# Where layer 1 of the first image stands in the order of emission: alone after layer 0, or in the second stream beside layer 0 of the next image

## The chip, the cores and the metric

The kernel runs on one core of one Trainium2 chip. A core has five engines with a queue of instructions each: TensorE (PE: matmuls, with weight loads as PEld), VectorE (DVE), ScalarE (ACT), GpSimd (POOL) and SyncE (SP), which here only starts transfers. The metric is the device time of one execution in microseconds (us); less is better. The time of a kernel is the median over its runs.

## The reference, cut to what matters

Four images of 48 channels and 256 x 256 pixels, all in float32, go through four layers. Each layer normalises its input over groups of three channels of the whole image (`_gn`), computes a branch and adds it to its input:

```python
x = x + _L0_conv_ref(_gn(x), ...)   # 1x1 and 3x3 conv to 288 channels, products of 8x8 spectra, layer norm, gate, 1x1 conv
x = x + _L1_conv_ref(_gn(x), ...)   # 1x1 conv to 288, mask on 8x8 spectra, 3x3 depthwise conv, gelu gate, 1x1 conv
x = x + _L2_conv_ref(_gn(x), ...)   # cumulative sums over the image, read at four corners of a box per pixel (gather)
x = x + _L3_conv_ref(_gn(x), ...)   # 1x1 and 3x3 conv to 192, gelu gate, 1x1 conv, mask on 8x8 spectra
```

The statistics of `_gn` cover a whole image, so a layer of one image can start only when the layer before of the same image has ended. Images do not depend on each other.

## The kernel before

**Two streams.** The work is a set of Python generators, one for each layer of each image (`layer0` to `layer3`), which emit instructions and `yield` a cost in planned units after each piece. `Net.run` holds two lists, `todo["a"]` and `todo["b"]`, and two planned clocks, `at["a"]` and `at["b"]`. It always advances the stream whose clock is behind and adds the yielded cost. So the emission is a zip of the two streams by planned cost. Stream a has the first statistics of image 0, then layers 0 and 1 of images 0, 1, 2, 3, then layer 3 of the four images. Stream b has the preparation of weights (`patch_weights`, `taps`), the first statistics of images 1 to 3, then layer 2 of the four images. A generator starts when its predecessors on the same image are done.

By the yields, layer 0 costs 1806 units (128 pieces, called units of layer 0 below, of two times 7), layer 1 costs 1429, layer 2 costs 3220, of which 316 are the sums and the first two pieces and the rest 33 pieces of four steps of 22 units, layer 3 costs 1080. Layer 2 of image 0 needs layer 1 of image 0, so stream b stands still while stream a emits layer 1 of image 0: that layer has the chip to itself. From then on layer 2 of image i lies beside layers 0 and 1 of image i+1, 3220 units against 3235, and layer 2 of image 3 beside layer 3 of images 0 to 2; layer 3 of image 3 (`layer3_pairs`) follows alone.

**What sets the order on an engine.** The emitted instructions go through a scheduler, which may move them within an engine by their priorities and its own estimate of times; an instruction passed to `self.pinned` (`keep_in_program_order`) keeps its place in the order of emission. After that each engine takes its instructions in order, and waits on semaphores for operands and for free buffers.

**Buffers.** Matmul results go to banks of PSUM. Stream a rotates through five banks of the pool `psa`, stream b through two of `psb`; one more bank (tag `w4`) holds the weights of the four corners in layer 2. Stream b allocates its SBUF tiles from the other side than stream a.

**Queues of transfers.** `self.dma` (line 238) starts the transfers of stream a on SP and those of stream b on POOL, where the gathers of layer 2 (line 1126, 16 a step) stand too. Layer 1 also starts many of its own on SP directly, pinned.

**Layer 0** makes, for each unit, 12 matmuls of 128 x 128 by 288 columns (line 399) and 4 of the rest of the rows (line 407) into four banks, copies them to `qkv` on ACT (line 483, four copies a unit), multiplies by the Fourier matrices (lines 491, 506), scales (lines 511 to 538), turns (line 544) and projects (line 556).

**Layer 1** has three passes. The first makes, for each of 16 strips, 32 matmuls of 49 rows by 288 columns (line 713), and copies each to the tile `hs` of which one strip (4608 KB) is stored to DRAM (`hD`). The copy is on DVE for every fourth result and on ACT for the others:

```python
if h and b % 2:
    nc.vector.tensor_copy(hs[:, :, h, b], ps[:, :288])
else:
    nc.scalar.copy(hs[:, :, h, b], ps[:, :288])
```

The second pass has 36 groups of eight channels: it loads a group (`hg`), makes the rims (line 771), sends them to neighbours by transfers (`yh<-yb`), and convolves and gates (lines 788, 794, 799, 800). The third turns back (line 865) and projects (line 877).

**Layer 2** makes the cumulative sums (lines 947, 968) and then 128 steps, each with half a piece of a 3 x 3 convolution (lines 1020, 1029), a projection (line 1045), 16 gathers (line 1126) into one of three tiles `V`, and their weighing and folding on DVE (lines 1138, 1146, 1148).

Of the kernel before, what the change touches and what calls it, by code (L numbers as in the profile page):

```python
# [192 lines left out]
class Net:  # L193
    def __init__(self, ctx, tc, a, out):
        self.tc, self.nc, self.a, self.out = tc, tc.nc, a, out
        self.nimage = a["x"].shape[0] // C

        self.banks = {
            f: ctx.enter_context(tc.tile_pool(name="ps" + f, bufs=n, space=PSUM)) for f, n in (("a", 5), ("b", 2))
        }  # L200
        self.stream, self.alone, self.turns = "a", False, 0
# [25 lines left out]

    def bank(self):
        if self.alone:
            self.turns += 1  # L230
# [160 lines left out]
    def convolve2(self, AB, W, n, j, to):  # L391
# [5 lines left out]
        def full(q, b):  # L397
            for g in range(3):
                nc.tensor.matmul(  # L399
                    to(q, b), A[:, j + half * q, 128 * b + g : 128 * b + g + 128], W[:, g, :],  # L400
                    start=b == 0 and g == 0, stop=b == 1 and g == 2,
                )

        def tails(b):
            for q in range(2):
                p = slice(64 * q, 64 * q + 58)
                nc.tensor.matmul(  # L407
                    to(q, b), B[p, j, 128 * b : 128 * b + 128], W[p, 3, :], start=b == 1, stop=b == 0
                )

# [31 lines left out]
    def layer0(self, x, mr, y, xb):  # L442
        nc, a = self.nc, self.a
        st = self.stat.tile([112, 129, 6], F32, name=self.nm("st"), tag="st" + self.stream, bufs=1)
        with ExitStack() as ctx:
# [39 lines left out]
            def spectra(t):  # L485
                t.t = []
                for f, c in ((self.fq, 0), (self.fk, 96)):
                    banks = [self.bank() for _ in range(2)]
                    for h in range(2):
                        p = slice(64 * h, 64 * h + 64)  # L490
                        nc.tensor.matmul(v3(banks[h]), f[p], t.qkv[p, :, c : c + 96], start=True, stop=True)  # L491
                    for h in range(2):
# [6 lines left out]
            def inverse(t):  # L499
# [5 lines left out]
                for h in range(2):  # L505
                    nc.tensor.matmul(po[64 * h : 64 * h + 64, 0:384], self.back[:, 0:64], t.t[h][:], start=True, stop=True)  # L506
                nc.scalar.copy(  # L507
# [33 lines left out]
            def turn(t):  # L541
                pt = self.bank()
                for b in range(4):
                    nc.tensor.transpose(pt[:96, 128 * b : 128 * b + 128], t.un[:, b, :], self.ident[:])
                t.u = sb.tile([96, 512], F32, name="u", tag=f"u{t.i}{t.j}", bufs=1)
                nc.scalar.copy(t.u[:], pt[:96, :])

            def project(t, other):
# [5 lines left out]
                for i, of in ((0, other), (1, t)):  # L554
                    n = 48 if i else 64
                    nc.tensor.matmul(pp[64 * i : 64 * i + n, :], pr[:, 0:n], of.u[:], start=True, stop=True)
                for q in range(2):
# [118 lines left out]
    def layer1(self, x, mr, y):  # L676
# [4 lines left out]
        with ExitStack() as ctx:  # L681
# [25 lines left out]
            for s in range(NS):  # L707
                xt = xts[s % 3]
                hs = sb.tile([128, 8 * NG, 2, 16], F32, name="hs", tag="hs")
                for b in range(16):  # L710
                    for h in range(2):
                        ps = self.bank()
                        nc.tensor.matmul(  # L713
                            ps[:, :288], xt[64 * h : 64 * h + 49, 128 * b : 128 * b + 128],
                            win[64 * h : 64 * h + 49], start=True, stop=True,
                        )
                        if h and b % 2:
                            nc.vector.tensor_copy(hs[:, :, h, b], ps[:, :288])
# [10 lines left out]
        with ExitStack() as ctx:  # L729
# [35 lines left out]
            def around(t):  # L765

                for e in range(4):
                    ps = self.bank()
                    for i in range(2):
                        c = 4 * i + e  # L770
                        nc.tensor.matmul(  # L771
                            ps[64 * i : 64 * i + 64, :].rearrange("p (s n) -> p s n", n=32),
                            t.wr[:, 64 * c : 64 * c + 64], t.hg[:, :, c, :], start=True, stop=True,
                        )
                    if e % 2:
# [8 lines left out]
            def gated(t, e):  # L784
                both = [self.bank() for _ in range(2)]
                for i in range(2):
                    c = 4 * i + e
                    nc.tensor.matmul(  # L788
                        both[i][:].rearrange("p (s n) -> p s n", n=32), t.wd[:, 128 * c : 128 * c + 128],
                        t.hg[:, :, c, :], start=True, stop=False,  # L790
                    )
                for i in range(2):
                    p = slice(64 * i, 64 * i + 64)
                    nc.tensor.matmul(  # L794
                        order(both[i][:]), t.wd[p, 1024 + 128 * e : 1152 + 128 * e], pick(t.yh, e)[p],
                        start=False, stop=True,
                    )
                gl = sb.tile([128, 512], F32, name="gl", tag="gl")
# [31 lines left out]
        with ExitStack() as ctx:  # L830
# [25 lines left out]
            def turn(s, j):  # L856
                gs, got = strips[s], []
                for q in range(3):
                    pt = self.bank()
                    for b in range(4):  # L860
                        if q < 2:
                            of = gs[:, 0:96, q, 4 * j + b]
                        else:
                            of = gs[:, 96:144, :, 4 * j + b].rearrange("p c h -> p (c h)")
                        nc.tensor.transpose(pt[:96, 128 * b : 128 * b + 128], of, self.ident[:])
                    gc = sb.tile([96, 512], F32, name="gc", tag=f"gc{q}")
# [4 lines left out]
            def project(s, j, got):  # L871
                xt, yt = buffers[s % 2]
                pp = self.bank()
                for last in range(2):
                    for h in range(2):
                        n = 48 if h else 64
                        nc.tensor.matmul(
                            pp[64 * h : 64 * h + n, :], pr[:, h if last else 2, 0:n], got[2 if last else h][:],
                            start=not last, stop=bool(last),
                        )  # L880
                whole = lambda t: t.rearrange("p (b r c) -> p b r c", b=4, r=8)
# [728 lines left out]
    def run(self, layers=(0, 1, 2, 3)):  # L1610
# [103 lines left out]
```

## Time and profile before

| what | value |
|---|---|
| median of 9 runs | 22758.85 us (22730.58 to 22847.83) |
| the profiled execution | 22663.54 us, span 22660.3 us |
| busy share PE, PEld, DVE, ACT, POOL | 81%, 48%, 47%, 27%, 37% |
| mean granted clock of TensorE | 0.851 |
| transfers | 3459.36 MB, mean 153 GB/s |
| layer 0 of image 0 | about 197 to 1849 us of the span |
| layer 1 of image 0, alone | about 1887 to 3056 us |
| layer 2 of image 0, first matmul of its sums to last gather | 3071 to 7549 us |
| layer 2 of image 3, last gather | 21693 us |

The profile is of one execution. A fp32 matmul of the program appears as two records on PE, so the counts of PE rows are twice those of the program. "Busy" is the time in which an engine had an instruction in work. The granted clock is the share of TensorE's full clock that the throttle granted. The chain of waits follows back from the last instruction what released what.

### The profile page before, as it was taken

What the parts mean: (1) busy time and instruction counts of PE and PEld (TensorE: products, weight loads), DVE (VectorE), ACT (ScalarE), POOL (GpSimd) and SP (SyncE); (2) the same over time, 40 slices, a digit from 0 to 9 for tenths busy, and PEclk for the clock granted to TensorE, in tenths of its full rate; (3) what the DMA queues carried; (4) which work ended last, traced back from release to release, by engine and by line L of the source; (5) the groups of instructions that cost most, each with busy time, mean ns of one, the idle gap of its engine ahead of it and who ended that gap; (6) DMA issues with size and microseconds to landing.
All of it is one profiled execution on the core that took longest, in us unless ns stands there. A gap on an engine that the chain in (4) does not pass through costs nothing.

```text
span 22660.3 us, 226381 instructions
## 1 busy us (share of the span) xinstructions
PE 18381.4 (81%) x78682; PEld 10914.8 (48%) x78682; DVE 10597.9 (47%) x23080; ACT 6045.2 (27%) x12781; POOL 8482.4 (37%) x8933
## 2 busy tenths in 40 slices
PE   8998898778777887787778877777878878877889
PEld 4564254444422544444224444442256656666678
DVE  4643244555444545554445455544443343343455
ACT  3445133333411333234113332331121111111122
POOL 1100004555444235455452354544522444444410
PEclk9998998888688988886889888868888888888889
DMA  6726863333777634336776433367864444444456
GB/s 173 165 60 226 274 200 98 100 98 96 222 249 239 187 98 103 97 97 205 247 250 191 107 101 95 97 195 245 250 204 118 106 104 108 105 106 106 105 130 150
DMA packets 1734597, 3459.36 MB, mean 153 GB/s; under 512 B 499598, under 2 KB 1273451, under 8 KB 1608600
## 3 DMA queue, kind: packets, MB, share of 16 engines
q1 hardware_dynamic: 1200800, 2149.26, 32.1%
q0 software_dynamic: 448688, 1098.99, 18.7%
q10 hardware_dynamic: 83968, 196.64, 3.4%
q8 instruction: 626, 10.26, 0.2%
q14 instruction: 515, 4.22, 0.1%
HBM read 2409.35 MB, written 832.39 MB: 143 GB/s over the span
## 4 chain that ended last, share of the span: by engine, by line
PE 61%; issue 10%; another core or an unknown queue 9%; DMA 9%; DVE 6%; ACT 2%; POOL 1%; SPq 1%; ACTq 0%; DVEq 0%; POOLq 0%
PE ps L399 19%; PE ps L1020 5%; PE ps L407 4%; PE ps L713 4%; PE ps L491 3%; PE ps L788 2%; PE ps L1045 2%; PE ps L1289 2%; DMA yh<-yb 2%; PE ps L771 2%; PE ps L794 2%; PE ps L506 2%; DVE V L1146 1%; POOL V L1126 1%
## 5 line engine op out<-in xcount | busy, mean ns | idle before, releaser
L1126 POOL DMA_INDIRECT V<-t,idx x8192 | 8049.0, 983 | 8221.5 <-DVE res L1148 4255.4
L399 PE MATMUL ps<-W,A 128*128 128x288 f32 (+1 forms) x21504 | 5464.5, 403 | 688.1 <-issue 471.7
L399 PEld LDWEIGHTS ps<-W,A 128*128 128x128 f32 x21504 | 4066.9, 205 | 2013.2 <-issue 1067.0
L1146 DVE TENSOR_TENSOR V<-V 128x1536 f32<-128x1536 f32 (+3 forms) x2048 | 1818.4, 888 | 9.2
L1138 DVE TENSOR_TENSOR V<-V,w 128x1536 f32<-128x1536 f32 x1024 | 1764.9, 1746 | 69.5 <-DMA V<-t,idx 38.0
L483 ACT COPY qkv<-ps 128x288 f32<-128x288 f32 x2048 | 759.0, 401 | 3468.1 <-PE ps L407 1085.9
L1020 PE MATMUL ps<-A,W 128*96 128x512 f32 x3072 | 1607.1, 661 | 61.3 <-issue 60.7
L511 DVE BATCH_NORM_STATS2 bs<-o 128x6 f32<-128x96 f32 x2048 | 381.7, 247 | 2443.4 <-ACT o L507 2001.1
L713 PE MATMUL ps<-win,xt 49*128 49x288 f32 x4096 | 1139.3, 610 | 405.4 <-ACT hs L720 217.6
L491 PE MATMUL ps<-qkv,c_dft_sb 64*128 64x384 f32 x4096 | 1061.4, 554 | 461.8 <-ACT qkv L483 240.1
L788 PE MATMUL ps<-hg,wd 128*128 128x512 f32 x2304 | 1217.5, 649 | 245.6 <-issue 73.2
L407 PE MATMUL ps<-W,B 58*128 58x288 f32 (+1 forms) x7168 | 1139.8, 413 | 241.0 <-issue 149.9
L1269 DVE TENSOR_TENSOR gp<-gl,ps 128x192 f32<-128x192 f32 x768 | 261.0, 351 | 2067.2 <-ACT gl L1268 1558.0
L238 POOL DMA_DIRECT2D X<-x x96 | 73.2, 763 | 2952.9 <-DMA x<-yt 2021.8
L800 DVE TENSOR_TENSOR hg<-gl,ps 128x512 f32<-128x512 f32 x576 | 394.4, 686 | 1542.6 <-ACT gl L799 815.9
L713 PEld LDWEIGHTS ps<-win,xt 49*128 49x128 f32 x4096 | 696.0, 269 | 824.1 <-ACT hs L720 406.0
L720 ACT COPY hs<-ps 128x288 f32<-128x288 f32 x1536 | 855.2, 676 | 845.4 <-PE ps L713 552.2
L1268 ACT ACTIVATE gl<-ps 128x192 f32<-128x192 f32 x768 | 246.1, 330 | 3060.0 <-PE ps L399 1318.4
L1020 PEld LDWEIGHTS ps<-A,W 128*96 128x96 f32 x3072 | 518.5, 181 | 1044.0 <-issue 1033.7
L407 PEld LDWEIGHTS ps<-W,B 58*128 58x128 f32 x7168 | 663.2, 195 | 644.9 <-issue 489.4
L794 PE MATMUL ps<-yh,wd 64*128 64x512 f32 x2304 | 741.0, 718 | 270.2 <-DMA yh<-yb 116.3
L799 ACT ACTIVATE gl<-ps 128x512 f32<-128x512 f32 x576 | 341.5, 597 | 2181.2 <-PE ps L794 1292.8
(226 smaller groups left out, 23254.0 us busy)
## 6 DMA issues: line engine op xcount, KB each, us to landing
hg<-hD SPq DMA_DIRECT2D x144, 2048.0 KB
hD<-hs SPq DMA_DIRECT2D x60, 4608.0 KB
gD<-hg SPq DMA_DIRECT2D x144, 1024.0 KB
gs<-gD SPq DMA_DIRECT2D x64, 2304.0 KB
V<-t,idx POOLq DMA_INDIRECT x8192
xt<-b SPq DMA_DIRECT2D x128, 896.0 KB
wd<-wD SPq DMA_DIRECT2D x144, 768.0 KB
A<-x SPq DMA_DIRECT2D x256, 387.0 KB
```

The source lines that it names most:

```text
L399: nc.tensor.matmul(to(q, b), A[:, j + half * q, 128 * b + g : 128 * b + g + 128], W[:, g, :], start=b == 0 and g == 0, stop=b == 1 and g == 2,
L407: nc.tensor.matmul(to(q, b), B[p, j, 128 * b : 128 * b + 128], W[p, 3, :], start=b == 1, stop=b == 0)
L483: nc.scalar.copy(t.qkv[:, 2 * q + b, :], banks[2 * b + q][:, 0:288])
L491: nc.tensor.matmul(v3(banks[h]), f[p], t.qkv[p, :, c : c + 96], start=True, stop=True)
L713: nc.tensor.matmul(ps[:, :288], xt[64 * h : 64 * h + 49, 128 * b : 128 * b + 128], win[64 * h : 64 * h + 49], start=True, stop=True,)
L720: nc.scalar.copy(hs[:, :, h, b], ps[:, :288])
L788: nc.tensor.matmul(both[i][:].rearrange("p (s n) -> p s n", n=32), t.wd[:, 128 * c : 128 * c + 128], t.hg[:, :, c, :], start=True, stop=False,
L794: nc.tensor.matmul(order(both[i][:]), t.wd[p, 1024 + 128 * e : 1152 + 128 * e], pick(t.yh, e)[p], start=False, stop=True,)
L1020: m = nc.tensor.matmul(to[q], W[:, g, :], A[:, 2 * q : 2 * q + 2, g : g + 256], start=q == 0 and g == 0, stop=q == 1 and g == 2,)
L1126: nc.gpsimd.indirect_dma_start(out=V[:, k, 4 * cr : 4 * cr + 4, :].rearrange("p e c -> p (e c)"), out_offset=None, in_=table, in_offset=ba ...
L1138: self.pinned(nc.vector.tensor_mul(Vm, Vm, wm.unsqueeze(2).to_broadcast([128, 32, 48])))
L1146: self.pinned(nc.vector.tensor_add(V[:, :, 0:n, :], V[:, :, 0:n, :], V[:, :, n : 2 * n, :]))
```

## The change

Layer 1 of image 0 moves from stream a to stream b, ahead of layer 2. Its planned cost is halved there (`pace`), so all its 1429 units are emitted beside 714 of the 1806 units of layer 0 of image 1, which in stream a now follows layer 0 of image 0 at once. The planned cost of layer 2 is multiplied by 0.96 for all images. While layer 1 stands in stream b (`crossed`):

- nearly all matmuls of both streams are pinned, so PE takes them in the order of emission;
- the two streams exchange their transfer queues: layer 0 of image 1 uses POOL's, layer 1 uses SP's;
- layer 1 has three banks instead of five: the two of `psb` and, every third time, the bank `w4`;
- the copies of the first pass are shared evenly: DVE for `h == 1`, ACT for `h == 0`.

```diff
     def bank(self):
+        if self.crossed and self.stream == "b":
+            self.turns += 1
+            if self.turns % 3 == 0:
+                return self.banks["b"].tile([128, 512], F32, name=self.nm("ps"), tag="w4", bufs=1)
         if self.alone:
...
     def dma(self, out, of):
-        (self.nc.sync if self.stream == "a" else self.nc.gpsimd).dma_start(out, of)
+        (self.nc.sync if (self.stream == "a") != self.crossed else self.nc.gpsimd).dma_start(out, of)
...
+    def pe(self, instruction):
+        return self.pinned(instruction) if self.crossed else instruction
...
-                        nc.tensor.matmul(v3(banks[h]), f[p], t.qkv[p, :, c : c + 96], start=True, stop=True)
+                        self.pe(nc.tensor.matmul(v3(banks[h]), f[p], t.qkv[p, :, c : c + 96], start=True, stop=True))
...
-                        if h and b % 2:
+                        if h and (b % 2 or self.crossed):
                             nc.vector.tensor_copy(hs[:, :, h, b], ps[:, :288])
...
-        a = [("first", 0)] + [(n, i) for i in images for n in (0, 1) if n in layers] + [(3, i) for i in images if 3 in layers]
+        early = (1, 0) if 1 in layers and len(images) > 1 else None
+        a = [("first", 0)] + [(n, i) for i in images for n in (0, 1) if n in layers and (n, i) != early]
+        a += [(3, i) for i in images if 3 in layers]
+        pace = {(2, i): 0.96 for i in images}
+        pace[early] = 0.5
         b = ([("weights", 0)] if 1 in layers else []) + ([("taps", 0)] if 3 in layers else [])
-        b += [("first", i) for i in images[1:]]
+        b += [("first", i) for i in images[1:]] + ([early] if early else [])
         b += [(2, i) for i in images if 2 in layers]
...
+            self.crossed = todo["b"][:1] == [early] and now["b"] is not None
             try:
-                at[f] += next(now[f])
+                at[f] += next(now[f]) * pace.get(todo[f][0], 1)
```

The other lines of the diff wrap the matmuls of layers 0 and 1 in `self.pe(...)`, as the one shown.

More of the change, by code (lines that the diff above doesn't have):

```diff
@@ L200, in __init__ @@
         }
-        self.stream, self.alone, self.turns = "a", False, 0
+        self.stream, self.crossed, self.alone, self.turns = "a", False, False, 0
         self.const = ctx.enter_context(tc.tile_pool(name="const", bufs=1))
@@ L398, in full @@
             for g in range(3):
-                nc.tensor.matmul(
+                self.pe(nc.tensor.matmul(
                     to(q, b), A[:, j + half * q, 128 * b + g : 128 * b + g + 128], W[:, g, :],
                     start=b == 0 and g == 0, stop=b == 1 and g == 2,
-                )
+                ))
         def tails(b):
@@ L406, in tails @@
                 p = slice(64 * q, 64 * q + 58)
-                nc.tensor.matmul(
+                self.pe(nc.tensor.matmul(
                     to(q, b), B[p, j, 128 * b : 128 * b + 128], W[p, 3, :], start=b == 1, stop=b == 0
-                )
+                ))
         for q in range(2):
@@ L505, in inverse @@
                 for h in range(2):
-                    nc.tensor.matmul(po[64 * h : 64 * h + 64, 0:384], self.back[:, 0:64], t.t[h][:], start=True, stop=True)
+                    self.pe(nc.tensor.matmul(po[64 * h : 64 * h + 64, 0:384], self.back[:, 0:64], t.t[h][:], start=True, stop=True))
                 nc.scalar.copy(
@@ L543, in turn @@
                 for b in range(4):
-                    nc.tensor.transpose(pt[:96, 128 * b : 128 * b + 128], t.un[:, b, :], self.ident[:])
+                    self.pe(nc.tensor.transpose(pt[:96, 128 * b : 128 * b + 128], t.un[:, b, :], self.ident[:]))
                 t.u = sb.tile([96, 512], F32, name="u", tag=f"u{t.i}{t.j}", bufs=1)
@@ L555, in project @@
                     n = 48 if i else 64
-                    nc.tensor.matmul(pp[64 * i : 64 * i + n, :], pr[:, 0:n], of.u[:], start=True, stop=True)
+                    self.pe(nc.tensor.matmul(pp[64 * i : 64 * i + n, :], pr[:, 0:n], of.u[:], start=True, stop=True))
                 for q in range(2):
@@ L712, in layer1 @@
                         ps = self.bank()
-                        nc.tensor.matmul(
+                        self.pe(nc.tensor.matmul(
                             ps[:, :288], xt[64 * h : 64 * h + 49, 128 * b : 128 * b + 128],
                             win[64 * h : 64 * h + 49], start=True, stop=True,
-                        )
-                        if h and b % 2:
+                        ))
+                        if h and (b % 2 or self.crossed):
                             nc.vector.tensor_copy(hs[:, :, h, b], ps[:, :288])
@@ L770, in around @@
                         c = 4 * i + e
-                        nc.tensor.matmul(
+                        self.pe(nc.tensor.matmul(
                             ps[64 * i : 64 * i + 64, :].rearrange("p (s n) -> p s n", n=32),
                             t.wr[:, 64 * c : 64 * c + 64], t.hg[:, :, c, :], start=True, stop=True,
-                        )
+                        ))
                     if e % 2:
@@ L787, in gated @@
                     c = 4 * i + e
-                    nc.tensor.matmul(
+                    self.pe(nc.tensor.matmul(
                         both[i][:].rearrange("p (s n) -> p s n", n=32), t.wd[:, 128 * c : 128 * c + 128],
                         t.hg[:, :, c, :], start=True, stop=False,
-                    )
+                    ))
                 for i in range(2):
                     p = slice(64 * i, 64 * i + 64)
-                    nc.tensor.matmul(
+                    self.pe(nc.tensor.matmul(
                         order(both[i][:]), t.wd[p, 1024 + 128 * e : 1152 + 128 * e], pick(t.yh, e)[p],
                         start=False, stop=True,
-                    )
+                    ))
                 gl = sb.tile([128, 512], F32, name="gl", tag="gl")
@@ L864, in turn @@
                             of = gs[:, 96:144, :, 4 * j + b].rearrange("p c h -> p (c h)")
-                        nc.tensor.transpose(pt[:96, 128 * b : 128 * b + 128], of, self.ident[:])
+                        self.pe(nc.tensor.transpose(pt[:96, 128 * b : 128 * b + 128], of, self.ident[:]))
                     gc = sb.tile([96, 512], F32, name="gc", tag=f"gc{q}")
@@ L876, in project @@
                         n = 48 if h else 64
-                        nc.tensor.matmul(
+                        self.pe(nc.tensor.matmul(
                             pp[64 * h : 64 * h + n, :], pr[:, h if last else 2, 0:n], got[2 if last else h][:],
                             start=not last, stop=bool(last),
-                        )
+                        ))
                 whole = lambda t: t.rearrange("p (b r c) -> p b r c", b=4, r=8)
```

## The prediction

> **What bounds the kernel now.** I read the slices of the page first, then the busy times of stages, then the groups of single stages, then the chain of waits. The slices (40 of 566.5 us; tenths busy, granted clock, transfers):
>
> ```profile
> PE   8998898778777887787778877777878878877889
> POOL 1100004555444235455452354544522444444410
> PEclk9998998888688988886889888868888888888889
> DMA  6726863333777634336776433367864444444456
> ```
>
> PE leads everywhere but is full nowhere except near the start; POOL's digits show where layer 2 gathers. Stages by busy time (columns: us, then PE, PEld, DVE, ACT, POOL with counts, clock, transfer share, GB/s):
>
> ```profile
> 1887.00:3071.00 1184.00, 1023.25 (x4048) 456.89 (x4048) 331.05 (x565) 431.57 (x795) 1.52 (x2) 0.91 0.88 287
> 1150.00:1800.00 650.00, 650.00 (x3054) 393.96 (x3053) 274.41 (x875) 305.66 (x763) 0.00 (x0) 1.00 0.21 58
> 3120.00:3451.00 331.00, 323.97 (x1410) 192.93 (x1407) 150.97 (x441) 126.23 (x302) 23.29 (x38) 0.99 0.53 142
> 3500.00:5600.00 2100.00, 1683.14 (x6490) 931.11 (x6490) 1133.49 (x2689) 656.71 (x1457) 1050.77 (x1062) 0.85 0.38 97
> 200.00:1150.00 950.00, 905.64 (x3903) 526.72 (x3902) 547.95 (x1901) 394.54 (x915) 157.61 (x262) 0.94 0.63 161
> ```
>
> From the top: layer 1 of image 0 alone (PE 86%), layer 0 alone (100%), layer 0 of image 1 beside the sums of layer 2 (98%), the same beside the gathers of layer 2 (80%, clock 0.85), layer 0 of image 0 beside the preparation of weights (95.3%). Two streams fill PE well, unless one of them is the gathering part of layer 2: there nothing is full, and PE stands idle a fifth of the time. Groups of three stages beside gathers (layer 0: 3500 to 5600; layer 1: 5700 to 6240; layer 3: 17300 to 20000) and the chain of the first:
>
> ```profile
> L483 ACT COPY qkv<-ps 128x288 f32<-128x288 f32 x423 | 155.7, 401 | 740.0 <-remote 270.3 <-PE ps L407 174.5 <-PE ps L399 134.4
> L1126 POOL DMA_INDIRECT V<-t,idx x1034 | 1038.4, 1004 | 1041.6 <-DVE res L1148 646.9 <-issue 299.2 <-DVE half L1063 45.5
> L1126 POOL DMA_INDIRECT V<-t,idx x272 | 261.5, 961 | 253.5 <-DVE res L1148 84.3 <-issue 77.4 <-DVE half L1065 56.4
> L1126 POOL DMA_INDIRECT V<-t,idx x1200 | 1153.6, 961 | 1389.9 <-DVE res L1148 569.0 <-issue 357.7 <-DVE w L1116 245.8
> by line: PE ps L399 25.2%; another core or an unknown queue 17.4%; issue 8.5%; PE ps L491 8.0%; PE ps L1020 7.6%; PE ps L407 5.3%; PE ps L506 3.6%; PE ps L1045 3.4%; PE ps L544 2.6%; PE ps L556 2.4%; DVE V L1146 2.3%; PE ps L1029 1.7%; DVE
> ```
>
> Four copies make a unit of layer 0: 423/4 = 105.75 units in 2100 us, 19.9 us each; alone it was 245 copies in 650 us, 10.6 us each. Sixteen gathers make a step of layer 2: 32.5 us beside layer 0, 31.8 beside layer 1, 36.0 beside layer 3. On the chain, matmuls of layer 0 are 25.2 + 8.0 + 5.3 + 3.6 + 2.6 + 2.4 = 47.1%, those of layer 2 about 13%; 25.9% is "issue" or unknown.
>
> **The change, part by part.** It turns two stages into one (layer 1 of image 0 with 51 units of layer 0 of image 1: 714 planned units of 14) and takes those 51 units from the stretch with layer 2, which before runs from 3071 to 21785 us. The sum has four terms.
>
> *1. The new stage.* PE work: 1023 us of layer 1 and 51 x 10.6 = 541 us of layer 0, together 1564. At the share of PE in layer 0 beside the preparation of weights, 95.3%, the nearest row of two streams without gathers, it takes 1640 us. Low end: layer 1's part at a clock of 0.98 in place of 0.91 (950 us) and 98% as beside the sums, 1520. High end: nothing overlaps, 1184 + 541 = 1725.
>
> The three banks add to that. Layer 1's first pass alone, with five banks:
>
> ```profile
> L713 PE MATMUL ps<-win,xt 49*128 49x288 f32 x1024 | 209.0, 516 | 41.0 <-ACT hs L720 39.4 <-DMA win<-win 1.1 <-DVE win L705 0.5
> L720 ACT COPY hs<-ps 128x288 f32<-128x288 f32 x384 | 199.5, 686 | 61.5 <-DMA hD<-hs 40.2 <-PE ps L713 20.8
> L718 DVE COPY hs<-ps 128x288 f32<-128x288 f32 x128 | 83.1, 650 | 167.1 <-PE ps L713 127.0 <-DMA hD<-hs 40.2
> ```
>
> A bank is held for a matmul and a copy. With 209/512 = 0.41 and 0.69 us that is 1.10 us, or 0.37 a result with three banks: below PE's 0.41, so no cost. With both records in full, 2 x 0.516 + 0.686 = 1.72 us, 0.57 a result: 512 x 0.16 = 84 us more. The order of emission puts 18 or 19 such matmuls in a row between two pieces of layer 0, too many for three banks to hide, so I take 40. In the other passes a bank is refilled after 1.0 to 3 us of other matmuls; nothing is added. The even copies move 128 from ACT (686 ns) to DVE (650 ns): ACT, 199.5 us busy of this pass's 253, falls to 256/384 of that, 133, DVE rises to 166. In the 14 units of layer 0 beside it ACT has 14 x 306/61 = 70 us more and DVE 63; both stay under 240 in a pass of some 400 us, so this is at nothing, and without that cover it would be PE's 39.4 us of waits for ACT that go.
>
> Strict order on PE means that a matmul which waits for a transfer holds back the other stream. Layer 1 alone has PE idle for transfers 32 us before line 771, 50 before 794, 10 before 788 and 18 before 865; these are inside the 1184 and so inside the high end. Transfers: 287 GB/s x 1184 us = 340 MB and 51 x 10.6 us x 58 GB/s = 31 MB, in 1640 us 226 GB/s, so the stores that layer 1 alone waits for get easier. Layer 0's loads move from SP to POOL, about 26 strips of 6 and some 20 more at the 763 ns of such a start there: 135 us on a POOL that is empty (1.52 us busy) until the sums, whose loads stand behind the last of them. SP keeps layer 1's transfers without those of the other stream.
>
> So 1680 us (1520 to 1809). Begun at 1887 as before, the stage ends at 3567, and layer 2 starts 3567 - 3071 = 496 us later (336 to 625).
>
> *2. The stretch with layer 2 gets 51 units of layer 0 less.* Bounds for one unit: 0 if layer 2's own steps set the pace, 47.1% x 19.9 = 9.4 if only its matmuls on the chain count, 10.6 as alone, 13.4 if it takes its share (47.1 of some 60) of the unnamed 25.9% too, 19.9 if both streams shrink in step. I take 12, between the two nearest rows: -612 us.
>
> *3. The end.* Planned, layer 2 of image 3 (4 x 3220 x 0.96 from 2632) now ends 134 units after layer 3 of image 2, 6 steps without company. A step alone cannot be shorter than its gathers, 16 x (0.983 busy + 0.30 between two in the timeline) = 20.5 us; in company it cost 32.5 less 1.57 x 12 of layer 0, so 14. +40 us (0 to 110).
>
> *4. The seam.* Layer 0 of image 1 began at 3119, after layer 1's end and its own loads; layer 2's sums now start beside running matmuls: -48 us (0 to -60). The pace of 0.96 changes only the mixture, and by a sum in which the streams add, nothing.
>
> Sum: 496 - 612 + 40 - 48 = -124 us on the profiled execution's own 22663.5 (the span and 3 us around it), 22540. The median of the runs lies 95 us above it, so 22635.
>
> **Two rules of the Trainium skill.** Layer 1 alone ran at a granted clock of 0.91, layer 0 alone at 1.00, layer 0 beside gathers at 0.85. "TensorE: Matmul & The Clock Gate", What's actually happening, says that the clock is halved by default and full after some 3.4 us of steady work; by it alone the 1023 us become 931, and the kernel gains some 95 us more. Against the change speaks the same page's A second HAM failure mode: PE that cycles through few banks idles briefly so often that the clock falls back. Row: the first pass ran at 0.81 with five banks already. If it stayed at one half, its 209 us would be 209 x 0.81/0.5 = 339, an estimate by that page, which takes back 130.
>
> **The rivals.**
> - *Layer 2 sets its own pace.* For it: a step takes about 32 us beside layer 0 as beside layer 1, and 36 beside layer 3, while the idle time of POOL ends mostly with DVE's line 1148, layer 2's own. Against it: gathers keep POOL only half busy, and matmuls of layer 0 are the largest share of the chain. It decides from a saving under (496 - 8)/51 = 9.6 us a unit. At half of my value, 6 us: +182, 22940; at nothing 23250.
> - *The stretch shrinks with PE's work.* Layer 0's matmuls there, by the groups of lines 399, 491, 407, 506, 544 and 556, are busy 744.9 + 221.5 + 153.8 + 112.2 + 78.8 + 75.1 = 1386 us, 13.1 a unit; over PE's 80% that is 16.4 a unit, -836: 22410.
> - *The gain is eaten in the new stage.* Strict order and three banks take it to 1809: -124 + 129, 22764, no change.
> - *The streams are not really side by side.* The built program's order on PE shows 16 matmuls of layer 0, then 16 to 20 of layer 1, and so on; I leave it out.
>
> **How the numbers follow.** Forecast about 22635: 0.37. PE's work: 0.20. No change: 0.11. Layer 2's pace: 0.32. About 0.2% (45 us) is what a measurement of this kernel can tell from no change. Faster 0.57, same 0.11, slower 0.32. The range reaches from below PE's case, 22330, to past the half-saving of the first rival, 23000; full lockstep and no saving at all stay outside.
>
> **What would show it.** In the profile after: the sums (lines of 947 and 968) of layer 2 start at about 3570 us with 51 units of layer 0 behind them (right if 3450 to 3650); PE is busy over 93% from 1890 to there at a clock over 0.95; a step of layer 2 falls from 32.5 to about 31.5 us beside layer 0; the last gather comes at about 21570, and layer 3 of image 3 takes as long as before. Wrong if steps stay at 32.5 or more, if PE's idle time before line 713 exceeds 100 us, or if the last gather comes after 21740.

## The result, and the profile after

The changed kernel takes 22911.5 us (median of 20 runs, 22861.9 to 22964.4). The kernel before, run beside it, took 22747.98 us: a ratio of 1.007 (1.006 to 1.0081), so it is 164 us slower where 124 us faster was forecast. The profiled execution is 22884.9 us, its span 22883.1 us, 222.8 us over the span of before (the difference of two single executions; the 164 us are of medians).

Later runs fell on chips of two kinds, and a time can't be read without that: on one kind the kernel before takes 22750 to 23060 us, on the other 18120. Stages without gathers last the same on both (layer 1 of image 0 alone 1161 to 1170 us, the first pass of the changed kernel 493 to 497 us); what differs is the stretch with layer 2, where a step takes about 32 or about 24 us. Every result below is held against the kernel before on its own chip, and the kinds are called "32 us" and "24 us".

Slices of the profile after (40 of 572 us):

```profile
PE   8999999776776797777777877767778878778769
POOL 1100000454454514545555145545541444444420
PEclk9997999886887898877888988778889888888889
DMA  6724665335786343347874433477755444444456
```

PE is at 9 from the second slice to the seventh, as meant. But the fourth, in which the new stage begins, has a clock digit of 7, and POOL gathers longer in the last slice but one (a digit of 2, where before had 1). By stages (us, PE, PEld, DVE, ACT, POOL with counts, clock, transfer share, GB/s):

```profile
1875.00:2375.00 500.00, 479.84 (x1684) 282.21 (x1684) 207.78 (x428) 220.13 (x409) 25.11 (x49) 0.72 0.56 183
2400.00:3270.00 870.00, 840.07 (x3012) 346.98 (x3012) 263.71 (x584) 290.12 (x561) 44.05 (x84) 0.99 0.72 227
3290.00:3640.00 350.00, 345.98 (x1876) 195.20 (x1873) 142.11 (x357) 158.99 (x340) 15.73 (x29) 0.99 0.61 196
1875.00:3642.00 1767.00, 1671.04 (x6592) 827.90 (x6592) 622.10 (x1389) 672.10 (x1315) 84.89 (x162) 0.90 0.65 210
4100.00:5250.00 1150.00, 906.00 (x3460) 500.76 (x3457) 625.13 (x1477) 352.53 (x777) 576.95 (x585) 0.84 0.37 95
21915.00:22066.00 151.00, 33.23 (x162) 25.61 (x163) 83.93 (x120) 5.47 (x9) 71.83 (x70) 0.59 0.41 104
2109.00:2122.00 13.00, 13.00 (x40) 6.49 (x38) 6.88 (x12) 7.19 (x14) 0.00 (x0) 0.50 0.31 71
```

The first three lines are the three passes of layer 1 of image 0, the fourth the whole stage: PE is busy 94.6% of it. Passes two and three run at a clock of 0.99, the first at 0.72. The fifth is layer 0 beside gathers, hardly changed from before: 569 gathers in 1150 us are 32.3 us a step (before 32.5). The sixth is the end of layer 2 of image 3 without company: 151 us in which PE has work for 33; 64 gathers, four steps, start in it. The last is one burst of layer 1 in the first pass, 40 records or 20 matmuls in 13 us: PE is busy throughout, at a clock of one half.

Groups of the first pass (lines have moved: 713 is now 720, the copy on DVE is 725, on ACT 727):

```profile
L720 PE MATMUL ps<-win,xt 49*128 49x288 f32 x1024 | 304.1, 602 | 17.3 <-ACT hs L727 8.6 <-DVE hs L725 5.3 <-DVE ln L531 1.6
L720 PEld LDWEIGHTS ps<-win,xt 49*128 49x128 f32 x1024 | 165.5, 248 | 149.9 <-ACT hs L727 67.6 <-DVE hs L725 54.6 <-issue 12.8
L725 DVE COPY hs<-ps 128x288 f32<-128x288 f32 x256 | 163.1, 645 | 148.8 <-PE ps L720 148.4
L727 ACT COPY hs<-ps 128x288 f32<-128x288 f32 x256 | 161.5, 647 | 135.5 <-PE ps L720 129.0 <-DMA aff<-L_beta 5.3
```

A record of the matmul takes 602 ns, where before it took 516. PE's own row shows 17.3 us of idle time; the wait stands one row lower, at the weight loads, which stand idle 149.9 us, 122.2 of it until a copy (on ACT or DVE) has emptied a bank. The copies in turn wait for matmuls. Three banks go round, and each side waits for the other.

The places that the forecast named: the sums of layer 2 start at 3642 us instead of 3071, that is 571 us later (forecast 496), with 208 copies of layer 0 before them, 52 units. The last gather starts at 22010 instead of 21693. The part after it is shorter, 873 us instead of 967. By the forecast's own signs, the start of the sums lies inside its 3450 to 3650 and PE is busy over 93%; but the clock of the stage is 0.90 and not over 0.95, a step stayed at 32.3 us instead of falling to 31.5, and the last gather lies past 21740, the one sign of being wrong that showed.

### The profile page after: what moved, and what is told of

Its sections match the earlier page's. It is cut to its first block, busy times and chain, and to the rows that moved or that the text cites. A ratio compares the mean times of both kernels' runs of the same rounds, so it can differ in the third digit from the quotient of the medians.

```text
span 22883.1 us, 226206 instructions
## 1 busy us (share of the span) xinstructions
PE 18368.1 (80%) x78682; PEld 10907.7 (48%) x78682; DVE 10674.4 (47%) x23208; ACT 5980.5 (26%) x12633; POOL 8557.3 (37%) x9106
## 5 line engine op out<-in xcount | busy, mean ns | idle before, releaser
L406 PE MATMUL ps<-W,A 128*128 128x288 f32 (+1 forms) x21504 | 5540.0, 406 | 770.2 <-issue 504.9
L414 PE MATMUL ps<-W,B 58*128 58x288 f32 (+1 forms) x7168 | 1192.5, 419 | 335.0 <-issue 216.4
L498 PEld LDWEIGHTS ps<-qkv,c_dft_sb 64*128 64x128 f32 x4096 | 445.4, 200 | 964.3 <-ACT qkv L490 447.3
```

The source lines that it names most:

```text
L406: self.pe(nc.tensor.matmul(to(q, b), A[:, j + half * q, 128 * b + g : 128 * b + g + 128], W[:, g, :], start=b == 0 and g == 0, stop=b == 1 ...
L414: self.pe(nc.tensor.matmul(to(q, b), B[p, j, 128 * b : 128 * b + 128], W[p, 3, :], start=b == 1, stop=b == 0))
L498: self.pe(nc.tensor.matmul(v3(banks[h]), f[p], t.qkv[p, :, c : c + 96], start=True, stop=True))
```

## The experiments

**Units taken out of the stretch, layer 1 left where it was.** `short_l0` is the kernel before without 48 of the 128 units of layer 0 of image 1 (12 of 32 strips, set by `cut` for that layer alone, whose input is passed on there, still loaded, stored and counted in the statistics), with layer 2's pace at 0.96; `short_pace`, `short_third` and `unit_32` are the same with 0.948, as shown. The rows that pass the input on are left out here.

```diff
-            for s in range(32):
+            for s in range(20 if self.cut else 32):
...
-                at[f] += next(now[f])
+                at[f] += next(now[f]) * (0.948 if todo[f][0][0] == 2 else 1)
...
```

> The kernel before with the pace of 0.96 for layer 2, in which layer 0 of image 1 computes 80 of its 128 units; for the other 48 it only passes its input on. So the stretch with layer 2 loses 48 units and no new stage is paid for. Forecast's term 2 (12 us a unit, 40 us for the end): 22750 - 576 + 40 = 22210 us. Theory that layer 2 has a floor of its own (a step alone takes about 21 us, so a unit saves (32.5 - 21)/1.57 = 7 us; 60 us for the end): 22750 - 336 + 60 = 22470. Theory that layer 2 alone sets the pace: 22750 or more.

> The kernel before, with 48 units of layer 0 of image 1 left out and layer 2's pace at 0.948, so that layer 2 has no steps alone at the end: what a unit taken from the stretch with layer 2 saves. Theory (a step without layer 0 still takes 20.5 to 22 us of its 32, so a unit saves about 7): 290 to 380 us under the kernel before. Rival (12 us a unit, as forecast): 576 us under it; rival (both streams shrink in step): 900.

> The kernel before without 48 units of layer 0 of image 1, pace of layer 2 at 0.948. Where a step of layer 2 takes 24 us: 386 us under the kernel before, as measured. Where it takes 32 us, theory (a step without company costs 20.5 to 22 us there too, so a unit of layer 0 saves about 7, and a little more as the chain's matmuls go): 320 to 430 us under it, a ratio of 0.981 to 0.986. Rival (12 us a unit as forecast): 576 us under, 0.975.

> The kernel before without 48 units of layer 0 of image 1, pace of layer 2 at 0.948. Where a step of layer 2 takes 32 us: theory (a step without company costs 20.5 to 22 us, so a unit saves 7 to 9): 320 to 430 us under the kernel before, a ratio of 0.981 to 0.986; rival (12 us a unit, as forecast): 576 us under it, 0.975. Where a step takes 24 us: 386 us under it as measured.

Measured at 24 us: ratios of 0.9798 (0.9783 to 0.9813), 0.9791 (0.9775 to 0.9807) and 0.9787 (0.977 to 0.9804). The last two are 386 and 388 us, 8.0 us a unit; by the last one's interval 7.4 to 8.7. At 32 us: 0.9781 (0.9757 to 0.9804), which is 493 us by the medians (22568.7 against 23061.7): 10.3 us a unit, 9.4 to 11.7 by the interval of the ratio. The loads, stores and statistics of the units stay and are not in this price; the two paces differ by nothing that can be measured (0.9798 and 0.9791). The forecast's 12 is outside the interval, and so are the 320 to 430 us of the theory that the runs were then meant to support, that layer 2's own gathers set a floor. Where the time went is seen in the gathers of layer 2's four images (us, busy POOL with count, clock, transfer share, GB/s), `unit_32` first, then the kernel before run again (`before_again`) on another chip of that kind:

```profile
3420.00:7567.00 4147.00, 2028.31 (x2048) 0.79 0.54 164
8006.00:12137.00 4131.00, 2022.68 (x2048) 0.80 0.54 162
12588.00:16676.00 4088.00, 2029.74 (x2048) 0.79 0.54 163
17218.00:21666.00 4448.00, 1965.32 (x2048) 0.81 0.42 104
```

```profile
3440.00:7643.00 4203.00, 2015.59 (x2048) 0.82 0.54 158
8127.00:12350.00 4223.00, 2011.46 (x2048) 0.80 0.53 156
12837.00:17059.00 4222.00, 2005.48 (x2048) 0.81 0.54 158
17583.00:22173.00 4590.00, 1964.93 (x2048) 0.82 0.43 103
```

The 48 units were taken from image 1, beside the gathers of image 0. Those gathers gain only 56 us; the next three gain 92, 134 and 142. With the units gone, layer 1 of image 1 starts at 4850 us instead of 5771, and lies beside layer 2 in their place. So the steps of image 0 keep company, and the gain comes later, spread over the other images. In sum it is near what a unit costs alone, 10.6 us, on this kind of chip; 8.0 us on the other kind is less, so that no run shows a rule in it.

> The kernel before once more, for a trace from the chip on which these runs are made (the first runs were some 25% faster there than the ones that the prediction was made from). If only stages with gathers differ, layer 1 alone still takes 1184 us, and a step of layer 2 takes 22 to 26 us in place of 32.

It took 23138.8 us in one run (23049.65 was the median on its chip), with steps of 33.0 us: it fell on a chip of the other kind than expected.

**Layer 2 without company.** `l2_alone` is the kernel before with layer 3 of images 0 to 2 held until layer 2 of image 3 has ended; all work is done.

```diff
-                    need = [before[n, i]] + ([("weights", 0)] if n == 1 else [("taps", 0)] if n == 3 else [])
+                    need = [before[n, i]] + ([("weights", 0)] if n == 1 else [("taps", 0), (2, 3)] if n == 3 else [])
```

> The kernel before, but layer 3 of images 0 to 2 waits for layer 2 of image 3, so the 128 steps of that layer stand alone and the layers 3 after it. If POOL's gathers are the floor of a step (16 x 1.28 us and little more), a step takes 20.5 to 22 us; if the chain over the three tiles V and VectorE's folds is, 27 to 32; the forecast's split (32.5 less 1.57 x 12) had 14, which POOL does not allow. Total at 21 us a step, with some 900 us for each layer 3 alone: about 23700 us.

20375.6 us in one run, 2256 over the kernel before (24 us chip). The stretch in question by busy times, and two of its groups:

```profile
14000.00:16700.00 2700.00, 722.93 (x2128) 342.51 (x2128) 1300.12 (x2185) 80.52 (x118) 2095.51 (x2043) 0.60 0.38 97
```

```profile
L1126 POOL DMA_INDIRECT V<-t,idx x1985 | 2066.0, 1041 | 604.7 <-issue 604.1 <-DMA V<-t,idx 0.6
L1138 DVE TENSOR_TENSOR V<-V,w 128x1536 f32<-128x1536 f32 x248 | 433.3, 1752 | 1101.4 <-DMA V<-t,idx 1058.8 <-issue 42.5
```

1985 gathers in 2700 us are 21.8 us a step, with POOL waiting for nothing but itself ("issue") and DVE for the gathers: the forecast's 20.5 us was near. On this kind of chip a step in company takes 24 us, so company is almost free for layer 2 there, and beside a step that has none PE stands idle nearly three quarters of the time (723 us of 2700 busy). No run shows a step without company on the other kind.

**A fourth bank.** `four_banks` is the changed kernel whose first pass takes every fourth bank from stream a's five.

```diff
-            if self.turns % 3 == 0:
+            if self.first and self.turns % 4 == 2:
+                return self.banks["a"].tile([128, 512], F32, name=self.nm("ps"), tag="ps")
+            if self.turns % 4 == 0 if self.first else self.turns % 3 == 0:
...
```

> The changed kernel, but in the first pass of layer 1 every fourth result goes to a bank of the other stream, so four banks in place of three. If the time a bank is held makes that pass 496 us long (0.685 us a result in a burst, clock 0.50), a result takes about 0.51 us and the clock rises: the pass falls to about 420 us, the kernel to 22840. If the strict order on TensorE or the copies make it long, the pass stays within 480 to 510 us.

18224.3 us, a ratio of 1.0061 (1.0045 to 1.0076) at 24 us; the changed kernel on such a chip gave 1.0119 (`after_third`, below). The first pass, the stage, and two groups of the pass (line 720 is 725 here):

```profile
1875.00:2260.00 385.00, 359.96 (x1696) 210.73 (x1696) 201.68 (x440) 211.08 (x410) 26.68 (x51) 0.90 0.72 238
1875.00:3524.00 1649.00, 1550.50 (x6604) 756.25 (x6604) 615.63 (x1400) 663.41 (x1316) 86.55 (x164) 0.96 0.70 225
```

```profile
L725 PE MATMUL ps<-win,xt 49*128 49x288 f32 x1024 | 202.3, 463 | 20.9 <-DVE hs L730 17.2 <-DVE ln L534 1.6 <-DVE win L715 0.5
L725 PEld LDWEIGHTS ps<-win,xt 49*128 49x128 f32 x1024 | 107.0, 196 | 115.2 <-DVE hs L730 81.6 <-ACT qkv L493 7.2 <-ACT hs L732 7.0
```

The same records in 379 us instead of 496 (493 in `after_third`; about 420 was expected); the clock is 0.90 instead of 0.72, a matmul record 463 ns instead of 602, and the sums start at 3524 instead of 3642 (3640). One bank is worth 116 to 118 us of this stage, and 110 us of the time by the medians of `four_banks` and `after_third`.

Single bursts show the two parts of this. First two stretches of one burst with three banks in the profile after, then a stretch with four in `four_banks`, and from each kind of burst one round of the banks at full clock:

```profile
2132.40:2136.00 3.60, 3.08 (x17) 1.70 (x16) 2.90 (x14) 2.56 (x5) 0.62 (x2) 1.00 1.10 384
2136.00:2142.00 6.00, 6.00 (x21) 4.20 (x22) 2.72 (x5) 3.15 (x5) 0.00 (x0) 0.54 0.11 31
2100.40:2107.40 7.00, 6.10 (x40) 3.31 (x40) 5.29 (x12) 5.62 (x10) 0.00 (x0) 1.00 0.07 26
```

```profile
2133.89 1.25 PE L720 MATMUL ps<-win,xt 49*128 49x288 f32 x6 [0.25 <-ACT hs L727]
2103.85 1.27 PE L725 MATMUL ps<-win,xt 49*128 49x288 f32 x8 [0.23 <-DVE hs L730]
```

At a clock of 1.00 a round takes some 1.49 us with either number of banks: work and an idle gap of some 0.25 us until a copy has ended. It yields three results, 0.50 us each, or four, 0.37 us each. With three banks the clock then falls to one half in the same burst, the gap is gone from PE's row, and a result takes about 0.65 us. So the fourth bank takes away both a wait and most of the time at half clock. What makes the clock fall is not shown: the gap in PE's row is as long with four banks, and there the clock stayed at 1.00 in this stretch.

**The first pass by itself.** `pass1_alone` emits the first pass alone with all eight banks, and 37 units beside the other two passes; `pass1_again` and `pass1_third` are the same kernel on two more chips.

```diff
-                        yield 3
+                        yield 0 if self.crossed else 3
...
+            if self.first:
+                k = self.turns % 8
+                if k < 5:
+                    return self.banks["a"].tile([128, 512], F32, name=self.nm("ps"), tag="ps")
...
```

> The changed kernel, but the first pass of layer 1 is emitted without layer 0 beside it and uses all eight banks; passes two and three stay beside 37 units of layer 0. Theory that the first pass spoils the new stage and that a unit of layer 0 is worth 7 us in the stretch: pass one falls from 496 to about 250 us (its stores then limit it), the stage from 1767 to about 1500, 14 units go back to the stretch (+98): 22911 - 267 + 98 = 22742 us, as the kernel before. By the forecast's 12 us a unit: 22911 - 267 + 168 = 22812.

> Layer 1's first pass by itself with all eight banks, 37 units of layer 0 beside its other two passes; the same kernel as before, wanted where a step of layer 2 takes 32 us. Theory (7 to 8 us saved a unit, 8.8 us spent on it in the new stage, the seam's 48 us won): 20 to 60 us under the kernel before, a ratio of 0.997 to 0.999. Rival (12 us a unit): 37 x (12 - 8.8) + 48 = 166 us under it, a ratio of 0.993.

> First pass by itself with eight banks, 37 units beside the other two passes. Where a step of layer 2 takes 24 us: 0.9985 to 0.999 of the kernel before, as measured twice. Where it takes 32 us: theory (7 to 8.5 us saved a unit) 0.996 to 0.999; rival (12 us) 0.993.

0.9985 (0.9976 to 0.9994), 0.999 (0.9981 to 0.9998) and 0.9981 (0.9972 to 0.999), all at 24 us: this one is faster than the kernel before, by 20 to 45 us. It did not run on a 32 us chip, so the bounds that were set for one are untested. Its first pass, and its stage:

```profile
1869.00:2116.00 247.00, 175.15 (x1072) 132.37 (x1072) 142.13 (x269) 140.58 (x260) 2.48 (x5) 0.81 0.99 341
1869.00:3385.00 1516.00, 1370.60 (x5960) 680.58 (x5960) 552.23 (x1217) 585.40 (x1152) 61.04 (x117) 0.94 0.74 240
```

Alone, the pass is bound by its stores (transfers 0.99), and more banks don't shorten it: 246 us, with five banks 250.

**The end without company.** `pace94` is the changed kernel with 0.948 for 0.96, so that layer 2 of image 3 ends beside layer 3.

```diff
-        pace = {(2, i): 0.96 for i in images}
+        pace = {(2, i): 0.948 for i in images}
```

> The changed kernel with 0.948 for 0.96 in layer 2, so that by plan layer 2 of image 3 ends with layer 3 of image 2 and no steps stand alone at the end. Theory that the 150 us of lonely steps are a real loss (6 steps at 22 to 24 us against the 10 to 14 us that they add in company): 60 to 90 us less than the changed kernel. Theory that the end costs nothing, since the stretch only gets the work back: within 20 us of it.

> The changed kernel on the chip of these runs. If its new stage is the same on both chips: first pass 496 us, stage 1767, and at 117 us more than with four banks (18224 us) about 18340, ratio 1.012. If the stage is also faster there, ratio 1.006.

At 32 us: the changed kernel 23205.0 us, 1.0081 (1.0052 to 1.011); `pace94` 23105.3 us, 1.0018 (1.0002 to 1.0034). By the medians the end was worth 100 us, by the ratios 145. `after_again` was expected on the 24 us kind and fell on the other. In the last stretch before its last gather (22164) PE has something to do, and the 151 us are gone:

```profile
22000.00:22164.00 164.00, 124.05 (x706) 105.55 (x706) 66.90 (x112) 19.18 (x47) 91.95 (x99) 0.79 0.44 108
```

**Both repairs.** `four_pace` and `both_32` are one kernel: the changed one with the fourth bank and 0.948.

> Both repairs at once: layer 1's first pass borrows a fourth bank, and the pace of layer 2 is 0.948 in place of 0.96. Theory (the two losses are separate: the first pass at half clock costs some 105 us, the end without company some 100): the first pass takes about 380 us in place of 493, layer 2 has no steps left alone at the end, and the time is some 200 us under that of the changed kernel, that is within 0.3% of the kernel before. Rival (12 us a unit, and the losses are all of what went wrong): 1 to 1.5% under the kernel before. Other rival (what one repair gains is given back in the stretch with layer 2, which sets its own pace): the first pass is shorter but the time stays at 1.002 of the kernel before or above it.

> A fourth bank for the first pass and layer 2's pace at 0.948. Where a step of layer 2 takes 32 us: theory (bank 105 us, end 100 us, each by itself): the changed kernel's 1.008 less 205 us, that is 0.997 to 1.001 of the kernel before; rival (12 us a unit and these two losses explain the whole miss): 0.988 to 0.994. Where a step takes 24 us: 1.001 as measured.

At 24 us 1.0011 (1.0002 to 1.002): 18129.9 us, about 205 under the changed kernel on another such chip. At 32 us 0.9967 (0.995 to 0.9983): 22991.5 against 23061.7, the best version measured there. Its stage is that of `four_banks`: 1875 to 3521 us, at a clock of 0.96. The rival of 12 us a unit (0.994 at most) is outside the interval. The other rival, that the stretch gives the gain back and the time stays at 1.002 or above, is at the upper end of the interval at 24 us and outside it at 32.

**Order and copies.** `unpinned` lets the scheduler move the matmuls of the new stage again (`pe` returns its instruction as it is); `old_copies` and `old_third` give DVE every fourth copy of the first pass again, as before the change.

```diff
-        return self.pinned(instruction) if self.crossed else instruction
+        return instruction
```

```diff
-                        if h and (b % 2 or self.crossed):
+                        if h and b % 2:
```

> The changed kernel without the strict order of emission on TensorE. If the strict order holds the streams up, the new stage falls by 50 us or more; if the banks are what limits the first pass, the pass stays within 20 us of 496 and the kernel within 40 us. If the scheduler's own order keeps layer 0 apart from layer 1, the stage gets longer: 1800 to 1900 us.

> The changed kernel with the copies of the first pass as they were, three on ACT for one on DVE. Theory (the first pass is long because PE runs at half clock with three banks; a copy is not what it waits for): the first pass takes 490 to 520 us as in the changed kernel, and the time is the same within 30 us of it, 1.006 to 1.010 of the kernel before. Rival (the bank is held by ACT's copies: 15 of 20 in a burst at 0.69 us are 10.4 us, near the burst's 13.8, and layer 0's own copies stand on ACT too): the first pass takes 560 us or more.

> The changed kernel with the first pass's copies as before the change. Theory: the first pass 10 to 20 us longer than the 493 of the changed kernel, and the time 5 to 30 us above it. Rival (even copies are worth much, since ACT holds the banks): 60 us or more above it.

> The changed kernel, beside the other three on one chip. Where a step of layer 2 takes 24 us: theory (7.6 us saved a unit, first pass at half clock, an end without company): 571 - 51 x 7.6 + 150 - 58 = 275 us over the kernel before by the terms read from the first pair of profiles, less some 30 as the tail's steps cost less there, that is a ratio of 1.011 to 1.016. Where it takes 32 us: 1.007 to 1.008 as measured twice. Rival (the saving a unit goes with the length of a step, 12 x 24/32 = 9 us): 571 - 459 + 150 - 58 = 204 on the first kind of chip, a ratio of 1.011 or less.

`unpinned`: 1.0081 (1.0052 to 1.0111) at 32 us, against 1.0081 for the changed kernel beside it. Its sums start 78 us later (3714 against 3636), with a first pass of 510 us against 493, yet the time is the same within the intervals. In part this is because 224 copies of layer 0 stand before its sums instead of 208: four more units are gone from the stretch, which at 10.3 us are 41 of the 78 us.

```profile
1875.00:2385.00 510.00, 498.71 (x1691) 291.42 (x1690) 207.24 (x422) 221.05 (x409) 23.22 (x45) 0.69 0.55 179
1875.00:3714.00 1839.00, 1770.08 (x6796) 868.87 (x6795) 648.54 (x1462) 707.57 (x1379) 83.49 (x159) 0.90 0.63 203
```

`old_third` and `after_third` on one chip (24 us): 1.0115 (1.0098 to 1.0132) and 1.0119 (1.0102 to 1.0137). The even copies shorten the first pass, from 510 to 493 us, but move the time by nothing that can be measured beside each other. `old_copies` on another 24 us chip gave 1.0131 (1.0115 to 1.0147), outside the 1.006 to 1.010 that were expected for the 32 us kind, and a first pass of 511 us, so the rival of 560 us or more is out. `after_third` lies inside the 1.011 to 1.016 of its theory; its interval holds the rival's 1.011 too, so it doesn't decide between them. In `old_copies` the pass has this group, the weight loads again waiting for copies:

```profile
L720 PEld LDWEIGHTS ps<-win,xt 49*128 49x128 f32 x1022 | 208.0, 262 | 119.4 <-ACT hs L727 79.5 <-DVE hs L725 14.8 <-issue 8.2
```

## Why the prediction was wrong, by its own steps

The forecast was -124 us, the result +164: 288 us apart. The time lies in the range, on the wrong side of no change. Three terms of the sum, all priced too kindly, make up most of it.

*Term 1, the new stage: 496 forecast, 571 measured (+75).* The stage lasts 1767 us instead of 1680 and begins 12 us earlier than assumed. The share of PE was right (94.6% against 95.3%), and so was the overlap: without the 118 us of the missing bank the stage lasts 1646 to 1649 us, where 1640 was forecast without a cost of the banks. That leaves little for the exchange of the queues, which had no run of its own. The step that failed is the price of three banks: 40 us taken, 116 to 118 us found by giving the fourth back. The estimate had two prices, 0.37 us a result (no cost) and 0.57 us with both records of a matmul in full (84 us), and took the middle, 40 us over PE's 0.41 or 0.49 a result. The price with both records in full was the right form: at full clock it is (2 x 0.40 + 0.65)/3 = 0.48 us, an estimate from the records (403 ns is their median with four banks) and the copy, and 0.50 is measured. The middle was right by luck, and only for as long as the clock is 1.00. What the sum left out is that the clock falls: at 0.50 the same estimate gives (2 x 0.68 + 0.65)/3 = 0.67 us (681 ns is the median of the records with three banks), and 0.65 is measured in the burst (20 in 13 us). Both prices used durations taken at a clock of 0.81, and the pass had 0.72.

The section of the Trainium skill that spoke against the change ("TensorE: Matmul & The Clock Gate", A second HAM failure mode) tells of a bf16 kernel whose matmuls cycle through banks, where PE idles briefly so often that the clock swings between one half and full. It names no number of banks; "few" is mine. The trace agrees on the swing: 1.00, then 0.54, within one burst. The warning was the better guide, but that its estimate of 130 us lies near the 118 is luck. The 130 were for all of the pass at one half and against the pass alone with five banks; in those terms the clock was 0.72 and PE's time in these matmuls rose from 209 to 304 us, by 95.

The same page's other rule, a full clock after some 3.4 us of steady work, was estimated at 95 us of gain for the stage. None came: the clock of the stage is 0.90, layer 1 alone had 0.91, with 0.99 in the second and third pass and 0.72 in the first. In the burst PE's row was busy for 13.00 of 13.00 us and the clock still at one half, so a full row is not enough to tell that the page's condition is met.

My sign that would have shown this wrong, PE idle for over 100 us before line 713, stayed quiet (17.3 us), since the wait is booked at the weight loads. "Perfetto Trace Analysis", Identifying the Most-Contended Engine, says that the matmul row's busy share is not a good measure of how close PE is to its limit, and to use the matmuls' own work and the busy share of the weight loads. The first half agrees with the rows above: 304 us busy and 602 ns with three banks, 202 us and 463 ns with four, for the same work. What pointed to the banks was not the weight loads' busy time but what ended their idle time: copies, for 122.2 us with three banks and 88.6 with four.

*Term 2, 51 units at 12 us: -612 forecast, -525 measured (+87, +15 to +133 by the interval).* The rival that put layer 2's pace at half of it, 6 us, came nearest in time (22940 against 22911), by luck and not by its mechanism: a unit saves 10.3 us (9.4 to 11.7) where the profile of before was taken, and 8.0 where steps are shorter. The step that failed is going above the bound "10.6 as alone", for a share of the unnamed 25.9% of the chain. A reading that fits, though no run shows it for the waits themselves: they stay when a unit goes, for the next layer's work moves up (in `unit_32` by 921 us) and has them as well. The bounds 9.4 (matmuls on the chain) and 10.6 both lie within the interval, so the runs don't choose between them; 8.0 lies under both. With 10.6 in place of 12 this term is -541, the sum -53 us, and with the stage's real length +22.

*Term 3, the end: 40 forecast, 100 measured by `pace94`.* There are 151 us without company, in which four steps of gathers start; six were planned. The step that failed is the price of company: 14 us a step, by 32.5 less 1.57 units at 12 us, rested on term 2, and it is layer 3 that is missing there and not layer 0. On the 24 us chips company costs a step only about 2 us (24 against 21.8), and there the fix of the end is worth 0.5% (1.0061 to 1.0011). How the 100 to 145 us at 32 us come about step by step stays open.

*Term 4, the seam: -48 forecast.* The sums of image 0 do reach their first gather in 355 us instead of 380. But the balance closes without the term: 571 - 525 + 100 = 146 against 164 (1.006 to 1.0081 is 136 to 184). With both repairs (sums at 3521 us) 3521 - 3071 - 525 = -75 against -70 us, and on the 24 us kind 452 - 51 x 8.0 = +44 against 20 by the ratio (4 to 36), which a unit at 8.5, inside its interval, would close. On the 32 us kind there is little room for 48 us more, and no run has the seam by itself.

*The rivals.* "Stretch shrinks with PE's work" (16.4 us a unit) is refuted by `unit_32`. "The gain is eaten in the new stage" was right in naming the banks and too low in what else is lost. Side by side the streams were: the fill of PE shows it. Strict order, which I had as a risk, shortens the stage by 78 us and the time by nothing that can be measured (`unpinned`), and the even copies are at nothing, as forecast.

Said in one line: a unit of layer 0 costs 8.9 us in the new stage with four banks (452/51), 11.2 with three (571/51), and saves 10.3 or 8.0 in the old place. There was little to win by moving it, and the banks and the end took more than that. The first theory after the result, a floor by layer 2's own gathers with 320 to 430 us for 48 units, fell with `unit_32` on the 32 us kind.

## What to carry to other kernels

Work that is moved between two places is worth the difference of two prices, so measure both: leaving the work out at its old place gives the one in a single run. Here the price "as alone" (10.6 us) was nearer to it than one with a share of unnamed waits (12) on the chips of the forecast, and too high on the others. When a stage has to share banks, look at the weight loads' waits and the granted clock beside PE's busy time; a full PE row can be PE at half its clock, as in the burst above. When two streams are zipped, check after every move that the long one still ends in company.

## What the runs showed of the hardware

- Chips differ by a quarter in the length of a step of layer 2 (32 and 24 us, two and three chips in the later runs), and by little in stages without gathers (layer 1 alone 1161 to 1170 us). From 3500 to 4900 us, layer 0 beside gathers, the same program has these two lines, first on the chip of the first profile, then in `l2_alone` (equal to the kernel before up to there):

```profile
3500.00:4900.00 1400.00, 1120.90 (x4356) 621.16 (x4356) 755.60 (x1791) 442.05 (x979) 692.94 (x698) 0.85 0.38 97
```

```profile
3500.00:4900.00 1400.00, 1374.52 (x6168) 793.49 (x6166) 1085.97 (x2567) 626.76 (x1386) 1064.08 (x1011) 1.00 0.55 139
```

  42% more matmuls in the same time, with PE at 98% and a full clock instead of 80% at 0.85; a POOL instruction takes about as long in both (0.99 and 1.05 us). What the slower kind waits for was not found.
- PE can be at a clock of 0.50 while its row is busy without a gap (13.00 of 13.00 us), in bursts of 49-row matmuls that go round three banks. The first pass had a clock of 0.72 with three banks and 0.90 with four.
- A round of the banks took 1.49 us at full clock with three banks and with four, so that a result cost 0.50 or 0.37 us.
